# A cross-attention and mixture-of-experts kernel: the order of its first loads, a projection in three passes, and new priorities in its opening list

## Chip, cores and metric

The kernel runs on one core of one Trainium2 chip. The metric is device microseconds for one execution of the whole program. The core has a matrix engine (TensorE, "PE" in the profile; its weight loads are "PEld"), a vector engine (VectorE, "DVE"), a scalar engine (ScalarE, "ACT"), a third elementwise engine (GpSimd, "POOL") and a queue engine (SyncE, "SP") that here only issues DMAs. ACT issues a few DMAs as well.

## What is computed

```python
x = x + xattn(layernorm(x), ctx, Wq, bq, Wk, bk, Wv, bv)
x = x + moe(layernorm(x), w_router, w_gating, w_gate, w_up, w_down)

# xattn: q = n @ Wq + bq; k = ctx @ Wk + bk; v = ctx @ Wv + bv
#        softmax(q k^T / 16) v, for each of the 16 batches
# moe:   combine weights from two softmaxes over 8 experts, then for each expert
#        (silu(n @ w_gate[e]) * (n @ w_up[e])) @ w_down[e], weighted and summed
```

x has 16 batches of 112 rows of 256; ctx has 16 batches of 375 rows of 256; each of the 8 experts has 1024 hidden columns. Everything is float32.

## The kernel before

The program has two parts. The **front** is the attention, the second layernorm, the router and the preparation of the first expert weights; it takes about the first 114 us. The **expert part** follows: 128 steps, each of seven block products (Strassen's scheme) of three matmuls, with the down projections between them.

The expert part does not multiply plain float32. Each operand is split into an upper part, rounded to a reduced format that the code calls fp32r, and a lower part, the rest. A product is three matmuls: upper by upper, upper by lower, lower by upper (`PASSES`; `prod`, L454, and `down_group`, L422). The attention's value projection (L1120) does the same. The other products of the front multiply plain float32, and the profile lists each of these matmuls as two instructions.

In the front, Wq and Wk are never applied to x and ctx one after the other. The kernel forms M = Wq Wk^T / 16 once: both weights are transposed on PE (`turned`, L863, tile `ps_w`), multiplied (`joined`, L877, tile `ps_m`), and scaled out of PSUM by ACT (L885) into `m_sb`. For each of four groups of four batches (g = 0 to 3), ACT and DVE normalize x to `xn`; PE transposes it (`turn`, L1001, tile `ps_xT`); ACT or DVE copies the transpose to `xnT_b` (by the helper at L740 to L742); PE multiplies it by M (`project`, L1014, tile `ps_qk`), in two halves `m` with two float32 matmuls of 448 columns each; ACT adds a bias and writes `qk` (L1023). Each batch b then has its ctx transposed (L1059, `ps_cT`), scores (L1071, `ps_sc`), a softmax on DVE and ACT, the transposed probabilities (L1092, `ps_pp`), their product with ctx (L1105, `ps_aa`), the value projection (L1120, `ps_po`), the residual and the second layernorm (L1127 to L1161), and one more transpose (L1167, `ps_xx`). `route(h)` computes the router's logits for half h of the rows (L1199, `ps_lg`) and what follows on ACT and DVE (L1210 to L1237); `split` forms upper and lower parts of the experts' input blocks (L295 on ACT, L298 on POOL).

The order of all this is not written out by hand. A planner, class `Line`, takes each operation with its engine (or a choice of two, `EITHER`), an estimated cost, a priority `pri`, what it reads and writes, and which ring buffers it needs. A load may be given an estimated landing time, `lands`. `Line.run` repeatedly takes the operation that can start first; among those of one engine that can start by then, the lowest `pri` wins. `LAG` is the estimated delay of a hand-over from another engine. The result is one fixed order per engine, which the hardware runs in order. The eight PSUM banks, and buffers for ctx, `xnT` and others, are such rings.

At the very start PE has nothing to multiply. It runs `WARM` = 7 matmuls on zeros (`idle`, L817), and up to `FILL` = 5 more of them are put where the planner sees a gap after the transposes of Wq. Loads of the start, in order of issue: SP has batches 0 and 1 of x (L799), Wq, Wk (L771), ctx of batches 0 and 1 (L794, L795), group 1 of x (L787), Wv; ACT has bq, bk and bv (L768) and then batches 2 and 3 of x (L799). Rows bq and bv are spread over all partitions by a matmul with ones and an ACT copy (`spread`, L839 and L841).

Of the kernel before, what the change touches and what calls it, by code (L numbers as in the profile page):

```python
# [30 lines left out]
class Line:  # L31


    LAG = {"PE": 0.2, "SP": 0.1}
    SECOND = 0.5

    def __init__(self, rings):
# [106 lines left out]
def kernel(  # L144
# [104 lines left out]
        + [ctx_t[7][:, m * GT : (m + 1) * GT]]  # L249
        for m in range(KC)  # L250
    ]
    xnT_b = [wide[6][:, k * GT : (k + 1) * GT] for k in range(KC)]
    x1_b = [wide[6][:TQ, KC * GT + i * D : KC * GT + (i + 1) * D] for i in range(3)]
    x1T = [wide[i].rearrange("p (k t) -> p k t", k=KC) for i in (2, 7)]
    s_b = [buf("s", [P, N], f"s{i}") for i in range(11)]
# [4 lines left out]
    wT = buf("d", [P, 2, KC, D], "wT")  # L260
    wv_hi, wv_lo = wv_b[:, 0], wv_b[:, 1]
    mix = buf("d", [P, 4, D], "mix")
    m_sb, bv_b, v_b = mix[:, :KC], mix[:, KC], mix[:, KC + 1]
    b_b = buf("rawd", [P, 2, D], "b_b")
    wv = buf("rawd", [P, KC, D], "wv")

# [530 lines left out]
    def load_x0(queue, i):  # L797
        t = own(xg_b, ("xg", 0))[0]
        queue.dma_start(t[:, i : i + 2, :], x[i : i + 2].rearrange("b t d -> t b d"))  # L799

    def x_loaded(g):
        if g:
            op("SP", 0.45 if g < 3 else 0.9, 4 * g - 6, lambda: load_x(g), new=(("xg", ("xg", g)),),
               waits=(("ctx", 5), ("ctx", 6)) if g == 3 else (), kb=448)
            return
        op("SP", 0.45, -22, lambda: load_x0(nc.sync, 0), writes=("x0",), new=(("xg", ("xg", 0)),), kb=224, lands=4.1)
        op("ACT", 0.45, -18, lambda: load_x0(nc.scalar, 2), writes=(("xg", 0),), kb=224, lands=5.5)

    def ctx_loaded(b):
        op("SP", 0.85, b - 3.5, lambda: load_ctx(b), new=(("ctx", ("ctx", b)),), kb=375)  # L810


    WARM, FILL = 7, 5

    def idle(k, n):
        for _ in range(n):
# [1 line left out]

    op("PE", 0.43 * WARM + 1.2, -50, lambda: idle(0, WARM), new=(("bank", ("idle", 0)),), writes=("warm",))
    x_loaded(0)  # L820
    load(-19, 256, lambda: weight(nc.sync, wn[:, 0], Wq), "wn0", lands=4.7)
    load(-18, 256, lambda: weight(nc.sync, wn[:, 1], Wk), "wn1", lands=7.0)
    load(-20, 1, lambda: row(nc.scalar, b_b[:, 0], bq), "bq0", queue="ACT", lands=3.0)
    load(-20, 1, lambda: row(nc.scalar, b_b[:, 1], bk), "bk0", queue="ACT", lands=3.3)
    load(-20, 1, lambda: row(nc.scalar, bv_b, bv), "bv0", queue="ACT", lands=3.6)
    op("ACT", 1.5, -16, lambda: nc.scalar.activation(warm, nhalf, AF.Exp), writes=("exp",))
    ctx_loaded(0)
    ctx_loaded(1)
    load(-1.9, 256, lambda: weight(nc.sync, wv, Wv), "wv")
    load(1.0, 16, load_router, "wr")  # L830
    for b in range(2, B):
# [4 lines left out]
    def spread(name, t, pri):  # L836

        k = ("b", name)
        op("PE", 0.45, pri, lambda: nc.tensor.matmul(bank(k, [P, D]), ones[:1], t[:1], start=True, stop=True),  # L839
           reads=(name + "0",), new=(("bank", k),))  # L840
        op("ACT", 0.38, pri, lambda: nc.scalar.copy(t, bank(k, [P, D])), reads=(k,), writes=(name,))  # L841

    spread("bq", b_b[:, 0], -24)
    spread("bv", bv_b, -23)

    def turn_bias():
        for j in range(KC):
# [24 lines left out]
    def joined(i):  # L872
        k = ("m", i)

        def join():
            for j in range(KC):
                nc.tensor.matmul(  # L877
                    bank(k, [P, D + 1]), wT[:, 0, j, i * P : (i + 1) * P], wk_b[:, j, :],
                    start=(j == 0), stop=(j == KC - 1),
                )  # L880

        op("PE", 0.87, -9, join, reads=["bkc"] + [("wT", s, j) for s in range(2) for j in range(KC)],
           new=(("bank", k),))
        op("ACT", 0.37, -9,
           lambda: nc.scalar.activation(m_sb[:, i, :], bank(k, [P, D + 1])[:, :D], AF.Copy, scale=SCALE),  # L885
           reads=(k,), writes=("m",))
        op("ACT", 0.2, -8,
           lambda: nc.scalar.activation(warm[:, i : i + 1], bank(k, [P, D + 1])[:, D:], AF.Copy, scale=SCALE),
           reads=(k, "exp"), writes=(("v", i),))
        op("DVE", 0.25, -5, lambda: nc.vector.tensor_scalar_mul(v_d[:, i, :], ident, warm[:, i : i + 1]),  # L890
           reads=(("v", i),), writes=(("vd", i),), port=True)
# [64 lines left out]

    def group(g):

        pri = 4 * g - 2.5 if g else -6
        at = slice(g * G, (g + 1) * G)  # L960
        xt = lambda i: x_at(g, i)

# [43 lines left out]
        for k in range(KC):  # L1006
            op("PE", 0.4, pri, lambda k=k: turn(k), reads=(("xn", g, 0), ("xn", g, 1)),
               new=(("bank", ("xT", g, k)),))
            op(EITHER, (0.54, 0.6), pri, lambda e, k=k: copy_on(e, xnT_b[k], bank(("xT", g, k), [P, GT])),
               reads=(("xT", g, k),), new=((f"xnT{k}", ("xnT", g, k)),))  # L1010

        def project(m):
            for k in range(KC):
                nc.tensor.matmul(  # L1014
                    bank(("qk", g, m, 0), [P, GT]), m_sb[:, k, m * P : (m + 1) * P], xnT_b[k],
                    start=(k == 0), stop=(k == KC - 1),
                )

        for m in range(KC):
            op("PE", 1.51, pri, lambda m=m: project(m), reads=("m", ("xnT", g, 0), ("xnT", g, 1)),  # L1020
               new=(("bank", ("qk", g, m, 0)),))
            op("ACT", 0.63, pri,
               lambda m=m: nc.scalar.activation(  # L1023
                   own(qk_b[m], ("qk", g, m)), bank(("qk", g, m, 0), [P, GT]), AF.Identity,
                   bias=r_sb[:, m : m + 1]),
               reads=(("qk", g, m, 0), "r"), new=((f"qk{m}", ("qk", g, m), (0, 1, 0, 2)[g]),),
               waits=(("ctx", 7),) if g == 3 else ())
# [6 lines left out]
            )  # L1034

        for i in range(G):
            op("DVE", 0.52, pri + 0.5, lambda i=i: bias(i), reads=(("xn", g, i // 2), "v"), writes=(("c0", g),),
               port=True)
        op("DVE", 0.22, pri + 0.5,
           lambda: nc.vector.tensor_scalar(cs[:TQ, at], cs[:TQ, at], bqk_b[:TQ], None, op0=ALU.add),  # L1040
# [2 lines left out]
    def batch(b):  # L1043
# [18 lines left out]
                )  # L1062

        for k in range(KC):
            op("PE", 0.33, b + 0.6, lambda k=k: turn(k), reads=(("ctx", b),), new=(("bank", ("cT", b, k)),))
            op(EITHER, (0.45, 0.53), b + 0.6, lambda e, k=k: copy_on(e, ctT(k), bank(("cT", b, k), [P, TK])),
               reads=(("cT", b, k),), new=(("ctT", ("ctT", b, k)),))

        def score():
# [3 lines left out]
                    start=(k == 0), stop=(k == KC - 1),  # L1073
                )

        op("PE", 1.33, b, score, reads=(("ctT", b, 0), ("ctT", b, 1), ("qk", g, 0), ("qk", g, 1)),
           new=(("bank", ("sc", b), *some),))
        op("DVE", 0.57, b,
           lambda: nc.vector.reduce_max(top(), bank(("sc", b), [TQ, TK]), axis=AX.X, negate=True),
# [27 lines left out]
                        start=(c == 0), stop=(c == NK - 1),  # L1107
                    )

        op("PE", 1.35, b, mix_ctx, reads=(("pT", b), ("ctx", b)), new=(("bank", ("aa", b), *some),))  # L1110
        op(EITHER, (0.36, 0.4), b, lambda e: copy_on(e, aT()[:, 0], bank(("aa", b), [P, KC, TQ])),
           reads=(("aa", b),), new=(("aT", ("aT", b)),))
        op("DVE", 0.41, b,
# [3 lines left out]
        def project():  # L1117
# [4 lines left out]
                        start=(k == 0 and s == 0), stop=(k == KC - 1 and s == 2),  # L1122
                    )

        op("PE", 0.75, b, project, reads=(("aT", b), ("aTl", b), "wvb"), new=(("bank", ("po", b), *some),))
        op("DVE", 0.5, b,
           lambda: nc.vector.scalar_tensor_tensor(  # L1127
               x1(), bank(("po", b), [TQ, D]), total[:TQ, col], x_at(g, i),
               op0=ALU.mult, op1=ALU.add),
# [18 lines left out]
        op("DVE", 0.95, b, stats, reads=(("x1", b),), writes=(("va1", b),))  # L1148
# [5 lines left out]
        def norm():  # L1154
# [8 lines left out]
        op("ACT", 0.55, b - 0.5, norm, reads=(("x1", b), ("nm1", b)), new=(("x1n", ("x1n", b)),))  # L1163

        def turn_x1():
            for k in range(KC):
# [4 lines left out]
        op("PE", 0.21, b, turn_x1, reads=(("x1n", b),), new=(("bank", ("xx", b), *some),))  # L1171
# [19 lines left out]
    def route(h):  # L1191

        key = ("lg", h)
        pri = (9.3, 21)[h]
        lg = lgs[h]

        def logits(j):
# [60 lines left out]
    route(0)  # L1258
    for h in range(NH):
        for i in (X_A11, X_A12):  # L1260
            split(h, i, (6.5, 28)[h], *early(h))
# [169 lines left out]
```

## Time and profile before

| | us |
|---|---|
| median of 3 runs | 962.53 (962.35 to 962.54) |
| the profiled execution | 962.02 |
| its span, first to last instruction | 960.24 |
| PE busy in the span | 954.9 |
| DVE, ACT, POOL busy | 646.9, 609.2, 376.5 |

The profiled execution is 0.5 us below the median, and 1.8 us of it lie outside the span. A matmul's end is modelled in this profile, and the durations of neighbouring matmuls overlap: what one of them costs is read from the distance of starts, or from the chain of waits, which puts one after the other. The busy time of the engines in the front, by stretches of it:

```profile
20.00:30.00 10.00, 10.00 (x64) 7.76 (x63) 7.20 (x27) 6.04 (x16) 4.18 (x6) 1.00 1.06 260
30.00:40.00 10.00, 10.00 (x74) 8.47 (x74) 6.68 (x30) 9.02 (x25) 4.69 (x7) 1.00 0.65 186
40.00:50.00 10.00, 10.00 (x62) 7.55 (x61) 8.28 (x31) 7.51 (x20) 4.46 (x6) 1.00 0.43 126
50.00:60.00 10.00, 10.00 (x73) 8.52 (x73) 5.19 (x18) 6.92 (x19) 3.35 (x4) 1.00 0.39 110
60.00:70.00 10.00, 10.00 (x86) 9.49 (x85) 7.83 (x29) 5.94 (x17) 2.11 (x3) 1.00 0.08 24
70.00:80.00 10.00, 10.00 (x59) 7.24 (x58) 8.85 (x27) 8.45 (x22) 7.28 (x9) 1.00 0.05 13
80.00:90.00 10.00, 10.00 (x74) 8.61 (x73) 7.76 (x31) 6.88 (x20) 7.76 (x13) 1.00 0.04 12
90.00:100.00 10.00, 10.00 (x74) 8.68 (x72) 7.65 (x26) 7.93 (x21) 9.84 (x16) 1.00 0.30 89
```

The columns are the stretch, its length, the busy time (and number of instructions) of PE, PEld, DVE, ACT and POOL, the granted PE clock, the share of the 16 DMA engines that was busy, and GB/s.

### The profile page before, as it was taken

Reading aid. Unit: us, or ns where it says so; the run is one execution under the profiler, and the core shown is the slowest. Engines: PE = TensorE matmul, PEld = TensorE weight load, DVE = VectorE, ACT = ScalarE, POOL = GpSimd, SP = SyncE. Lnnn points to the kernel's source line nnn. Section 1 sums busy time; section 2 is a strip of 40 time slices with the busy share of each in tenths; the row PEclk is TensorE's granted clock in tenths of the full one; section 3 lists DMA queues with packets and bytes.
Section 4 is the critical chain, followed back from the end, with each engine's and each line's share of the span. In section 5 each row is a group of like instructions: output and inputs, shape, how many; then the busy total and the mean of one; then the engine's idle time right before and its main releaser. Section 6 shows DMA issues by size and latency. Waiting matters only on the chain.

```text
span 960.2 us, 16096 instructions
## 1 busy us (share of the span) xinstructions
PE 954.9 (99%) x6066; PEld 894.2 (93%) x6066; DVE 646.9 (67%) x1290; ACT 609.2 (63%) x1241; POOL 376.5 (39%) x481
## 2 busy tenths in 40 slices
PE   9999999999999999999999999999999999999998
PEld 5887899999999999999999999999999999999998
DVE  4868686777675666756676757667666767566675
ACT  4867776666666666666556665666566666666553
POOL 3428963444315443344334333543244431544000
PEclk9999999999999999999999999999999999999999
DMA  8621201011101110011100110111001110100001
GB/s 225 183 70 38 64 23 34 23 34 45 34 12 33 33 45 23 12 34 44 34 23 24 36 41 23 34 34 33 23 24 33 44 33 12 33 24 12 19 21 39
DMA packets 36067, 38.65 MB, mean 40 GB/s; under 512 B 3267, under 2 KB 33990, under 8 KB 35990
## 3 DMA queue, kind: packets, MB, share of 16 engines
q1 hardware_dynamic: 35744, 37.40, 13.4%
q8 instruction: 47, 0.77, 0.4%
q14 instruction: 30, 0.25, 0.1%
q10 hardware_dynamic: 246, 0.23, 0.1%
HBM read 33.95 MB, written 1.84 MB: 37 GB/s over the span
## 4 chain that ended last, share of the span: by engine, by line
PE 99%; DVE 0%; issue 0%; ACT 0%
PE pd L422 32%; PE pC L454 16%; PE pE L454 16%; PE pA L454 16%; PE pB L454 8%; PE ps_aa L1105 2%; PE ps_sc L1071 2%; PE ps_qk L1014 1%; PE ps_po L1120 1%; PE ps_cT L1059 1%; PE ps_lg L1199 1%; PE ps_idle L817 1%; PE ps_pp L1092 1%; PE ps_xx L1167 0%; PE ps_xT L1001 0%; PE ps_m L877 0%
## 5 line engine op out<-in xcount | busy, mean ns | idle before, releaser
L422 PE MATMUL pd<-wd,hhi 128*128 128x256 f32 x1792 | 311.2, 277 | 0.0
L422 PEld LDWEIGHTS pd<-wd,hhi 128*128 128x128 f32 x1792 | 275.9, 188 | 1.9
L422 PE MATMUL pd<-wd,hlo 128*128 128x256 f32 x896 | 248.4, 277 | 0.0
L454 PE MATMUL pC<-xs_hi,w 128*128 128x448 f32 x508 | 184.8, 364 | 0.1
L454 PE MATMUL pE<-xs_hi,w 128*128 128x448 f32 x508 | 184.5, 363 | 0.0
L454 PE MATMUL pA<-xs_hi,w 128*128 128x448 f32 x504 | 183.3, 364 | 0.0
L357 POOL TENSOR_TENSOR w<-raw,w 128x384 fp32r<-128x384 f32 x64 | 78.4, 1225 | 265.4 <-ACT w L347 265.4
L422 PEld LDWEIGHTS pd<-wd,hlo 128*128 128x128 f32 x896 | 168.4, 188 | 0.0
L648 ACT COPY pB<-pA 128x448 f32<-128x448 f32 x122 | 63.8, 523 | 104.0 <-PE pA L454 104.0
L366 POOL TENSOR_TENSOR wd<-rawd,wd 128x512 fp32r<-128x512 f32 x32 | 41.5, 1298 | 180.1 <-ACT wd L364 180.1
L454 PEld LDWEIGHTS pC<-xs_hi,w 128*128 128x128 f32 x508 | 95.3, 188 | 10.9 <-DVE s_1c L568 0.5
L454 PEld LDWEIGHTS pE<-xs_hi,w 128*128 128x128 f32 x508 | 95.4, 188 | 6.9 <-ACT pE L585 0.4
L454 PEld LDWEIGHTS pA<-xs_hi,w 128*128 128x128 f32 x504 | 94.6, 188 | 5.6
L658 ACT COPY pE<-pB 128x448 f32<-128x448 f32 x122 | 63.1, 517 | 54.2 <-DVE s_6s L528 0.8
L454 PE MATMUL pC<-xs_lo,w 128*128 128x448 f32 x254 | 91.9, 362 | 0.0
L454 PE MATMUL pE<-xs_lo,w 128*128 128x448 f32 x254 | 91.5, 360 | 0.0
L454 PE MATMUL pB<-xs_hi,w 128*128 128x448 f32 x252 | 91.4, 363 | 0.0
L454 PE MATMUL pA<-xs_lo,w 128*128 128x448 f32 x252 | 90.7, 360 | 0.0
L357 POOL TENSOR_TENSOR w<-tt,w 128x512 fp32r<-128x512 f32 x64 | 88.0, 1375 | 0.1
L454 PEld LDWEIGHTS pE<-xs_lo,w 128*128 128x128 f32 x254 | 47.6, 187 | 3.4
L454 PEld LDWEIGHTS pB<-xs_hi,w 128*128 128x128 f32 x252 | 47.3, 188 | 3.1
L454 PEld LDWEIGHTS pC<-xs_lo,w 128*128 128x128 f32 x254 | 47.6, 187 | 2.5
(1453 smaller groups left out, 1772.0 us busy)
## 6 DMA issues: line engine op xcount, KB each, us to landing
raw<-in_L_ffn_w_gate_dram SPq DMA_DIRECT2D x32, 256.0 KB
raw<-in_L_ffn_w_up_dram SPq DMA_DIRECT2D x32, 256.0 KB
rawd<-in_L_ffn_w_down_dram SPq DMA_DIRECT2D x32, 256.0 KB
ctx<-in_ctx_dram SPq DMA_DIRECT2D x13, 336.0 KB
out_dram<-acc SPq DMA_DIRECT2D x6, 256.0 KB
wide<-in_ctx_dram SPq DMA_DIRECT2D x3, 336.0 KB
wide<-in_x_dram SPq DMA_DIRECT2D x2, 448.0 KB
ctx<-in_ctx_dram SPq DMA_DIRECT2D x13, 39.0 KB
```

What stands on the lines that cost most here:

```text
L357: nc.gpsimd.tensor_sub(wts[k][1][:, d], w, f(wts[k][0][:, d]))
L366: nc.gpsimd.tensor_sub(wds[q][1], rawds[q], f(wds[q][0]))
L422: nc.tensor.matmul(pd, hs[a][:, t * P : (t + 1) * P], wds[q][w][:, fi, :], start=(opening and s == 0), stop=(last and s == 2), skip_group_ ...
L454: nc.tensor.matmul(ps, w_[w][:, wi, :], (xs_hi, xs_lo)[a][h][xi], start=(start and s == 0), stop=(stop and s == 2), skip_group_check=True,)
L648: nc.scalar.copy(pb, pa)
L658: nc.scalar.copy(pe, pb)
L817: nc.tensor.matmul(bank(("idle", k), [P, 512]), zero[:, :P], zero, start=True, stop=True)
L1014: nc.tensor.matmul(bank(("qk", g, m, 0), [P, GT]), m_sb[:, k, m * P : (m + 1) * P], xnT_b[k], start=(k == 0), stop=(k == KC - 1),)
L1059: nc.tensor.transpose(bank(("cT", b, k), [P, TK])[:, c * KT : (c + 1) * KT], ct()[:, c, k * P : (k + 1) * P], ident[:KT, :KT],)
L1071: nc.tensor.matmul(bank(("sc", b), [TQ, TK]), own(qk_b[k], ("qk", g, k))[:, i * TQ : (i + 1) * TQ], ctT(k), start=(k == 0), stop=(k == KC ...
L1092: nc.tensor.transpose(bank(("pp", b), [KT, NK, TQ])[:, c, :], p()[:, c * KT : (c + 1) * KT], ident[:TQ, :TQ])
L1105: nc.tensor.matmul(bank(("aa", b), [P, KC, TQ])[:, k, :], ct()[:, c, k * P : (k + 1) * P], pT()[:, c, :], start=(c == 0), stop=(c == NK - 1),)
```

## The change

**Loads.** Wq moves from SP to ACT, ahead of bq and bk there. Batches 2 and 3 of x move from ACT to SP, ahead of Wk. bv is no longer loaded as a row and spread by PE and ACT; one DMA on SP, after ctx of batch 1, writes it to all 128 partitions. The estimated landing times of bq and bk become later, and the spread of bq gets the priority of the bk step beside it.

**Zero matmuls.** `WARM` goes from 7 to 8, `FILL` from 5 to 6.

**The queries' projection.** M and the transposed `xn` are each held as an upper and a lower part, in tiles that the expert part uses only later. ACT writes M's upper part, DVE its lower part. The copy of the transpose becomes the upper part, and a new DVE operation per transpose writes the lower part. `project` runs six matmuls in place of two float32 ones (which the profile lists as four instructions), for each of two halves in each of four groups.

**The planner's numbers.** The PE hand-over is taken as 0.15 for 0.2, and a number of priorities change; the later ones among them are the turns of ctx, the scores and the first router step, the earlier ones most of what ends a batch.

```diff
-    LAG = {"PE": 0.2, "SP": 0.1}
+    LAG = {"PE": 0.15, "SP": 0.1}
...
-    xnT_b = [wide[6][:, k * GT : (k + 1) * GT] for k in range(KC)]
+    xnT_b = [[t[1][5 + k][:, :GT] for t in (xs_hi, xs_lo)] for k in range(KC)]
+    m_b = [[t[1][3 + k][:, :D] for t in (xs_hi, xs_lo)] for k in range(KC)]
...
-        op("ACT", 0.45, -18, lambda: load_x0(nc.scalar, 2), writes=(("xg", 0),), kb=224, lands=5.5)
+        op("SP", 0.45, -22, lambda: load_x0(nc.sync, 2), writes=(("xg", 0),), kb=224, lands=5.5)
...
-    WARM, FILL = 7, 5
+    WARM, FILL = 8, 6
...
-    load(-19, 256, lambda: weight(nc.sync, wn[:, 0], Wq), "wn0", lands=4.7)
+    load(-21, 256, lambda: weight(nc.scalar, wn[:, 0], Wq), "wn0", queue="ACT", lands=4.7)
     load(-18, 256, lambda: weight(nc.sync, wn[:, 1], Wk), "wn1", lands=7.0)
-    load(-20, 1, lambda: row(nc.scalar, b_b[:, 0], bq), "bq0", queue="ACT", lands=3.0)
-    load(-20, 1, lambda: row(nc.scalar, b_b[:, 1], bk), "bk0", queue="ACT", lands=3.3)
-    load(-20, 1, lambda: row(nc.scalar, bv_b, bv), "bv0", queue="ACT", lands=3.6)
+    load(-20, 1, lambda: row(nc.scalar, b_b[:, 0], bq), "bq0", queue="ACT", lands=4.4)
+    load(-20, 1, lambda: row(nc.scalar, b_b[:, 1], bk), "bk0", queue="ACT", lands=5.2)
...
+    load(-2.2, 128, lambda: nc.sync.dma_start(bv_b, bv.rearrange("(o d) -> o d", o=1).to_broadcast([P, D])), "bv")
...
-    spread("bq", b_b[:, 0], -24)
-    spread("bv", bv_b, -23)
+    spread("bq", b_b[:, 0], -9.7)
...
-           lambda: nc.scalar.activation(m_sb[:, i, :], bank(k, [P, D + 1])[:, :D], AF.Copy, scale=SCALE),
-           reads=(k,), writes=("m",))
+           lambda: nc.scalar.activation(m_b[i][0], bank(k, [P, D + 1])[:, :D], AF.Copy, scale=SCALE),
+           reads=(k,), writes=(("mh", i),))
+        op("DVE", 0.42, -9,
+           lambda: nc.vector.scalar_tensor_tensor(
+               m_b[i][1], bank(k, [P, D + 1])[:, :D], SCALE, f(m_b[i][0]), op0=ALU.mult, op1=ALU.subtract),
+           reads=(k, ("mh", i)), writes=("m",))
...
+            op("DVE", 0.54, pri,
+               lambda k=k: nc.vector.tensor_sub(xnT_b[k][1], bank(("xT", g, k), [P, GT]), f(xnT_b[k][0])),
+               reads=(("xT", g, k), ("xnT", g, k)), writes=(("xnl", g, k),))
 
         def project(m):
             for k in range(KC):
-                nc.tensor.matmul(
-                    bank(("qk", g, m, 0), [P, GT]), m_sb[:, k, m * P : (m + 1) * P], xnT_b[k],
-                    start=(k == 0), stop=(k == KC - 1),
-                )
+                for s, (a, w) in enumerate(PASSES):
+                    nc.tensor.matmul(
+                        bank(("qk", g, m, 0), [P, GT]), m_b[k][a][:, m * P : (m + 1) * P], xnT_b[k][w],
+                        start=(k == 0 and s == 0), stop=(k == KC - 1 and s == 2),
+                    )
 
         for m in range(KC):
-            op("PE", 1.51, pri, lambda m=m: project(m), reads=("m", ("xnT", g, 0), ("xnT", g, 1)),
+            op("PE", 1.21, pri, lambda m=m: project(m),
+               reads=("m", *(("xnT", g, k) for k in range(KC)), *(("xnl", g, k) for k in range(KC))),
...
```

The priorities, `pri` before and after (b is the batch, g the group):

| operation | before | after |
|---|---|---|
| normalization, transposes, projection of group g > 0 | 4g - 2.5 | 4g - 3.0 |
| key-bias sums of a group (DVE) | pri + 0.5 | pri + 1.0 |
| turn of ctx, on PE | b + 0.6 | b + 1.3 |
| scores, on PE | b | b + 0.6 |
| probabilities by ctx (L1105) | b | b - 0.4 |
| residual, its statistics (DVE) | b | b - 0.3 |
| second layernorm (ACT) | b - 0.5 | b - 1.0 |
| transpose of its result (L1167) | b | b - 0.5 |
| router of the first half | 9.3 | 13.5 |
| first two splits of the first half | 6.5 | 8 |

More of the change, by code (lines that the diff above doesn't have):

```diff
@@ L262 @@
     mix = buf("d", [P, 4, D], "mix")
-    m_sb, bv_b, v_b = mix[:, :KC], mix[:, KC], mix[:, KC + 1]
+    bv_b, v_b = mix[:, KC], mix[:, KC + 1]
     b_b = buf("rawd", [P, 2, D], "b_b")
@@ L957, in group @@
     def group(g):
-        pri = 4 * g - 2.5 if g else -6
+        pri = 4 * g - 3.0 if g else -6
         at = slice(g * G, (g + 1) * G)
@@ L1008, in group @@
                new=(("bank", ("xT", g, k)),))
-            op(EITHER, (0.54, 0.6), pri, lambda e, k=k: copy_on(e, xnT_b[k], bank(("xT", g, k), [P, GT])),
+            op(EITHER, (0.54, 0.6), pri, lambda e, k=k: copy_on(e, xnT_b[k][0], bank(("xT", g, k), [P, GT])),
                reads=(("xT", g, k),), new=((f"xnT{k}", ("xnT", g, k)),))
+            op("DVE", 0.54, pri,
+               lambda k=k: nc.vector.tensor_sub(xnT_b[k][1], bank(("xT", g, k), [P, GT]), f(xnT_b[k][0])),
+               reads=(("xT", g, k), ("xnT", g, k)), writes=(("xnl", g, k),))
         def project(m):
             for k in range(KC):
-                nc.tensor.matmul(
-                    bank(("qk", g, m, 0), [P, GT]), m_sb[:, k, m * P : (m + 1) * P], xnT_b[k],
-                    start=(k == 0), stop=(k == KC - 1),
-                )
+                for s, (a, w) in enumerate(PASSES):
[3 more added lines that the diff above has]
+                    )
         for m in range(KC):
-            op("PE", 1.51, pri, lambda m=m: project(m), reads=("m", ("xnT", g, 0), ("xnT", g, 1)),
+            op("PE", 1.21, pri, lambda m=m: project(m),
+               reads=("m", *(("xnT", g, k) for k in range(KC)), *(("xnl", g, k) for k in range(KC))),
                new=(("bank", ("qk", g, m, 0)),))
@@ L1036, in group @@
         for i in range(G):
-            op("DVE", 0.52, pri + 0.5, lambda i=i: bias(i), reads=(("xn", g, i // 2), "v"), writes=(("c0", g),),
+            op("DVE", 0.52, pri + 1.0, lambda i=i: bias(i), reads=(("xn", g, i // 2), "v"), writes=(("c0", g),),
                port=True)
@@ L1064, in batch @@
         for k in range(KC):
-            op("PE", 0.33, b + 0.6, lambda k=k: turn(k), reads=(("ctx", b),), new=(("bank", ("cT", b, k)),))
+            op("PE", 0.33, b + 1.3, lambda k=k: turn(k), reads=(("ctx", b),), new=(("bank", ("cT", b, k)),))
             op(EITHER, (0.45, 0.53), b + 0.6, lambda e, k=k: copy_on(e, ctT(k), bank(("cT", b, k), [P, TK])),
@@ L1074, in score @@
                 )
-        op("PE", 1.33, b, score, reads=(("ctT", b, 0), ("ctT", b, 1), ("qk", g, 0), ("qk", g, 1)),
+        op("PE", 1.33, b + 0.6, score, reads=(("ctT", b, 0), ("ctT", b, 1), ("qk", g, 0), ("qk", g, 1)),
            new=(("bank", ("sc", b), *some),))
@@ L1108, in mix_ctx @@
                     )
-        op("PE", 1.35, b, mix_ctx, reads=(("pT", b), ("ctx", b)), new=(("bank", ("aa", b), *some),))
+        op("PE", 1.35, b - 0.4, mix_ctx, reads=(("pT", b), ("ctx", b)), new=(("bank", ("aa", b), *some),))
         op(EITHER, (0.36, 0.4), b, lambda e: copy_on(e, aT()[:, 0], bank(("aa", b), [P, KC, TQ])),
@@ L1123, in project @@
                     )
-        op("PE", 0.75, b, project, reads=(("aT", b), ("aTl", b), "wvb"), new=(("bank", ("po", b), *some),))
-        op("DVE", 0.5, b,
+        op("PE", 0.75, b + 0, project, reads=(("aT", b), ("aTl", b), "wvb"), new=(("bank", ("po", b), *some),))
+        op("DVE", 0.5, b - 0.3,
            lambda: nc.vector.scalar_tensor_tensor(
@@ L1146, in stats @@
             nc.vector.tensor_scalar_mul(nm1[:TQ, col], mv1[:TQ, b, 0:1], -1.0)
-        op("DVE", 0.95, b, stats, reads=(("x1", b),), writes=(("va1", b),))
+        op("DVE", 0.95, b - 0.3, stats, reads=(("x1", b),), writes=(("va1", b),))
         op("POOL", 0.56, b - 4,
@@ L1162, in batch @@
            reads=(("rs1", b),), writes=(("nm1", b),))
-        op("ACT", 0.55, b - 0.5, norm, reads=(("x1", b), ("nm1", b)), new=(("x1n", ("x1n", b)),))
+        op("ACT", 0.55, b - 1.0, norm, reads=(("x1", b), ("nm1", b)), new=(("x1n", ("x1n", b)),))
         def turn_x1():
@@ L1169, in turn_x1 @@
                 )
-        op("PE", 0.21, b, turn_x1, reads=(("x1n", b),), new=(("bank", ("xx", b), *some),))
+        op("PE", 0.21, b - 0.5, turn_x1, reads=(("x1n", b),), new=(("bank", ("xx", b), *some),))
         h, at = divmod(b, HB)
@@ L1193, in route @@
         key = ("lg", h)
-        pri = (9.3, 21)[h]
+        pri = (13.5, 21)[h]
         lg = lgs[h]
@@ L1260 @@
         for i in (X_A11, X_A12):
-            split(h, i, (6.5, 28)[h], *early(h))
+            split(h, i, (8, 28)[h], *early(h))
     for n, i in enumerate((X_S1, X_S2, X_S3, X_S4)):
```

## Prediction

> **What bounds the kernel now.** I read the page first: who is busy, and what ended last.
>
> ```profile
> PE 954.9 (99%) x6066; PEld 894.2 (93%) x6066; DVE 646.9 (67%) x1290; ACT 609.2 (63%) x1241; POOL 376.5 (39%) x481
> ...
> PE 99%; DVE 0%; issue 0%; ACT 0%
> ```
>
> PE is on the chain for 99% of the span. The waits listed for PE agree: apart from 1.2 us at the start they name two, of 0.4 and 0.2 us. So time comes from PE's work, from PE's start, and from the few breaks in its chain. The change touches only the front, so next I read the chain of waits in order of time from 0 to 119 us. Columns: start, us, what.
>
> ```profile
> 1.19 3.17 PE ps_idle L817 x7
> 4.36 1.15 PE ps_b_bq L839 x2
> 5.50 0.85 PE ps_b_bv L839 x2
> 6.36 1.05 PE ps_w L863 x4
> 7.40 0.94 PE ps_bk L848 x4
> 8.34 2.26 PE ps_idle L817 x5
> 10.61 0.04 issue
> 10.65 1.11 PE ps_w L863 x4
> ...
> 16.63 3.01 PE ps_qk L1014 x8
> ...
> 34.71 1.51 PE ps_qk L1014 x4
> ...
> 110.10 0.63 DVE s_0u L1320
> 110.73 0.02 issue
> 110.76 0.63 DVE s_0c L1320
> 111.39 0.04 issue
> 111.43 0.88 PE ps_first_C L454 x3
> ```
>
> From 10.65, where Wk's transposes begin, the chain is PE alone up to 110.08. Behind that lie breaks of 2.2 us: three DVE additions of 0.63 and an ACT copy of 0.35 (112.63). A matmul saved between 10.65 and 110 is therefore saved in the end, as long as PE stays fed.
>
> **The projection on PE.** On the chain the four groups' `ps_qk` cost 3.01, 1.51 + 1.52, 1.52 + 1.52 and 3.01: 12.09 us for 32 instructions, 0.377 each. The new form, fp32r of 128x448, stands in the trace: the chain has "PE pA L454 x3" at 0.60 throughout the first expert steps, 0.20 each. Four groups by two halves by six are 48, or 9.6 us. Entering such a block from float32 costs something: on the chain the first blocks between float32 work took 0.62, 0.70, 0.62 and 0.72, on average 0.06 to 0.07 over 0.60. For eight blocks that is 0.5 us, for four (halves back to back) 0.25. Saving: 12.09 - 9.6 = 2.5 at best, 2.0 at worst; I take **2.1**.
>
> [...] The rows say 2.5: an fp32r matmul of 448 columns costs 0.20, not half of 0.377. [...]
>
> **What the projection adds elsewhere.** DVE gets eight subtractions of 128x448, PSUM less SBUF. The nearest row is L1320, an addition with one operand in PSUM in the same shape, 614 to 622 ns: 5.0 us. Two lower parts of M, 128x256, are like L1127 (112x256, 0.48): 1.0. Together 6.0 us on DVE, of which the table above shows 44.0 us busy between 20 and 80, so 16 idle. This hides as a sum, but not everywhere: in 70 to 80, where group 3 is projected, DVE has 8.85 and ACT 8.45, and 1.2 more makes ten of ten. Against that the router of the first half leaves this stretch (L1214 to L1237, nine DVE operations of 0.17 to 0.34, about 2.2 us), as its priority becomes 13.5. I cost DVE's load at nothing.
>
> As a delay, each group's projection starts a subtraction (0.62) and a hand-over later. What covers it is PE work that needs neither: turns of ctx (0.32 each), `ps_pp` (0.32), `ps_aa` (1.33). In group 1 the last copy of the transpose ended at 34.30 and the matmuls began at 34.55, so the delay would show there if nothing else were ready; in group 3 the copies ended at 72.88, the matmuls began at 73.68. Cost with cover: nothing. Without it: 4 x 0.65 = 2.6 us.
>
> **The start.** WARM + 1 adds 0.43: the loads of L817's weights stand 0.43 apart (1.59, 2.02, 2.44, 2.87). bv's spread goes: -0.85. FILL + 1 adds 0.43 again. Wq's transposes and bk keep their price. Sum: 0.43 - 0.85 + 0.43 = 0.0, and Wk's transposes begin at 10.65 once more, if Wk is there and all six zero matmuls are placed ahead of it. Was it Wk or the fill that PE waited for?
>
> ```profile
> PEld ps_w L863 <- PE ps_idle L817: 1.0, 1, 1.0
> ```
>
> In the list of waits of the first 20 us the name is that of the zero matmuls, not of a DMA. So Wk landed no later than that, and the fill is what sets 10.65.
>
> *DMA.* Ahead of Wk the same 960 KB must pass (x in two parts of 224, Wq, Wk of 256 each), in another order: SP issues x's second part at 1.20 in Wq's place, Wk at 1.67 as before, Wq goes out on ACT at 0.73 and is needed after bq's spread, near 5.9. Worst case: x's second part, so far shared between two queues (it landed at 8.7, where DVE's L909 starts), goes wholly ahead of Wk, 224 KB at the 250 GB/s of this stretch, 0.9 us. Best case: none, even a gain if not all fills are placed: down to -0.9. I take 0, by the wait row. x's second part lands earlier, which lets DVE's statistics start earlier, but PE is not waiting for them.
>
> *bq and bk* now stand behind Wq in ACT's queue. PE reads bq at 4.8, and the order puts bk behind Wq's transposes. Should bq be late, PE waits in order, and the six fills behind it move along: at most 0.5.
>
> *bv's DMA* is 128 KB: 0.5 us of DMA time, on a stretch where the DMA share is about 1.0. Behind it on SP stand group 1's x, Wv and the later ctx. SP also waits for landings (3.2 us before 8.71, for x), so Wv and x may issue some us later than 4.6 and 5.0. Who waits: group 1's statistics (14.7, wanted for a projection at 34), Wv's cast (17.0, wanted at 31), ctx of batch 2 (turned after 19.6). Nobody soon: nothing. Uncovered: 0.5. POOL reads bv first at 18.96.
>
> *The clock.* [...]
>
> ```profile
> L877 PE MATMUL ps_m<-wide,wT x8: 378/380/670, 11.8 to 13.6; 128*128 128x257 f32 x8
> ```
>
> One of eight took 670 ns, the other seven 380. With the same pattern ending at the same 10.65 I expect the same moment, near 12.3. [...]
>
> **Priorities.** They add no work. With PE gapless from 10.65 to 110 they can only make gaps or move those behind 110. Later turns and scores and earlier ends of batches shorten the way to the last batch, and the router's 28 logits of the first half (2.8 us on PE between 61 and 71) become work that can fill a gap later. On the other side fewer turned ctx lie ready when PE wants one. The 2.2 us of breaks behind 110 come from the expert part's first additions, which stay. Bounds: -1.5 to +1.5; value: 0.
>
> **Sum.** 960.2 - 2.1 = 958.1 for the span; 1.8 outside makes 959.9 against the profiled execution's 962.0. The median lies 0.5 above that: **960.4**. Its own range is 958.9 to 961.9. What can be told from no change here is 0.2%, 1.9 us, so the border to faster is at 960.6, and this forecast lies close by it.
>
> **Rivals.**
> *Breaks go as well (958.2).* The priorities remove half or all of the 2.2 us behind 110. For it: PE would have logits left over. Against it: those additions wait for products in a fixed sequence.
> *Given back (962.6).* PE saves 2.1 but waits for the lower parts, 2.6 uncovered at worst less some cover, or the start slips by 0.9 and the breaks grow. For it: group 1's 0.25 us between copy and matmul. Against it: five cT turns followed in a row at 24.4, so PE has spare work as a rule.
> *DVE becomes the bound (966.4), slower.* In the front all softmax, residual and statistics work goes through DVE in one fixed order; 6.0 us added to it and shown in full give 960.4 + 6.0. It decides from the point where 4.1 of the 6.0 are exposed. For it: 70 to 80 is full, and POOL reaches 9.84 of 10 behind it. Against: 16 us idle between 20 and 80, and `EITHER` copies can go to ACT.
>
> **Numbers.** Forecast 0.50 (0.34 of it below 960.6, 0.16 within 0.2%); breaks gone too 0.16 (all faster); given back 0.16 (0.04 faster, 0.09 same, 0.03 slower); DVE 0.18 (all slower). Faster 0.54, same 0.25, slower 0.21. The range reaches down to 957.4 (breaks gone, and 0.8 of the start's possible gain) and up to 965.0, where 4.6 of DVE's 6.0 us are exposed; some 0.15 to 0.2 lies outside, most of it DVE's case in full.
>
> **What would show it.** Right: `ps_qk` on the chain near 2.4 us a group; Wk's transposes near 10.65; PE with no new waits up to 108; the last `ps_first` blocks some 2 us earlier. Wrong: PE waiting for DVE ahead of L1014 or in batches; a later 10.65; M's product at half rate; or longer breaks at 108 to 116.

## The result and the profile after

The changed kernel is slower. Its median is 965.52 us (22 runs, 962.40 to 969.97); the kernel before, run beside it on the same chip, has 962.47 (22 runs, 959.56 to 962.90). The ratio is 1.004, with a 95% interval of 1.0029 to 1.0051.

The times of the changed kernel fall into two groups with nothing between 964.3 and 966.7: 11 runs from 962.4 to 964.3, and 11 from 966.8 to 970.0. So the median is no run's time; it lies halfway across the gap, and one run more in either group would move it by more than 1 us. The kernel before has two groups as well, closer together (5 runs from 959.6 to 960.7, 17 from 962.0 to 962.9), and its profile is of the upper one. The profiled execution of the changed kernel, 963.12 with a span of 961.1, is from its lower group, so its profile can show only part of the loss. The upper group needed a profile of its own (below).

First the page of the changed kernel: busy time of the engines, and the chain's shares.

```profile
PE 952.0 (99%) x6082; PEld 896.9 (93%) x6082; DVE 658.5 (69%) x1298; ACT 609.4 (63%) x1242; POOL 377.5 (39%) x481
...
PE 98%; DVE 2%; issue 0%; ACT 0%; DVEq 0%; ACTq 0%
```

PE is busy 2.9 us less (954.9 before), and the span is 0.9 us longer: PE now waits somewhere. DVE's share of the chain went from nothing to 2%, and DVE is busy 11.6 us longer, where the prediction's sum was 6.0. The list of PE's waits gives the place (columns: who waited for whom; us in total, times, longest):

```profile
PE ps_xx L1177 <- DVE total L1109: 3.4, 1, 3.4
```

There was no such wait before. The timeline there (start, us, engine, line, operation, tile written and read, shape):

```profile
85.17 0.55 POOL L1160 TENSOR_TENSOR rs<-rs,nhalf 112x1 f32<-112x1 f32 x1
...
85.47 4.75 DVE L1225 TENSOR_TENSOR lg<-lg,lmx 128x112 f32<-128x112 f32 x1
85.69 1.00 POOL L359 TENSOR_TENSOR w<-raw,w 128x384 fp32r<-128x384 f32 x1
...
88.82 1.26 POOL L359 TENSOR_TENSOR w<-tt,w 128x512 fp32r<-128x512 f32 x1
90.04 0.49 POOL L334 TENSOR_TENSOR tt<-raw 128x128 f32<-128x128 f32 x1
...
90.14 0.53 DVE L744 COPY s<-ps_cT 128x375 f32<-128x375 f32 x1
...
90.82 0.61 PE L1177 MATMUL ps_xx<-ident,x1n 112*128 112x112 f32 x2 [3.36 <-DVE total L1109]
```

One DVE instruction takes 4.75 us. It is the router's subtraction for the first half, over 112 columns; its twin in the kernel before (L1215) took 0.28 at 71.2. Both instructions of that line, and POOL beside the first, in the kernel before:

```profile
70.48 0.92 POOL L1150 TENSOR_TENSOR rs<-rs,nhalf 112x1 f32<-112x1 f32 x1 [2.67 <-DVE nm L1146]
...
71.24 0.28 DVE L1215 TENSOR_TENSOR lg<-lg,lmx 128x112 f32<-128x112 f32 x1
71.37 0.73 POOL L996 TENSOR_TENSOR ctx<-ctx,mix 112x256 f32<-112x256 f32 x1
...
114.27 1.44 DVE L1215 TENSOR_TENSOR lg<-lg,lmx 128x112 f32<-128x112 f32 x1
114.29 1.29 POOL L357 TENSOR_TENSOR w<-tt,w 128x512 fp32r<-128x512 f32 x1
```

After the change it began while a short POOL instruction was running, and ended when the four L359 instructions behind that on POOL, 85.69 to 90.1, were done. (L359 is L357 of the kernel before.) POOL itself went on without a gap, with L334 at 90.04. And in the kernel before POOL was not idle at 71.24 either, yet the subtraction was not held there; beside L357 at 114.27 it was. So it matters what POOL runs, not only that it is busy: 0.28 us beside L1150 and L996, 1.44 beside L357. Behind the held subtraction, in DVE's fixed order, stand a reciprocal (`total`, L1109) and copies that PE wants, and so PE is idle for 3.4 us.

What follows the idle time costs more. Busy time by stretch (columns as in the table of stretches before: PE, PEld, DVE, ACT, POOL, then the granted PE clock):

```profile
84.00:88.00 4.00, 3.46 (x25) 2.74 (x24) 3.86 (x8) 3.63 (x10) 3.92 (x7) 1.00 0.14 37
88.00:92.00 4.00, 1.18 (x6) 1.04 (x7) 3.96 (x7) 0.40 (x2) 3.92 (x7) 0.83 0.38 123
92.00:96.00 4.00, 4.00 (x22) 3.59 (x22) 3.30 (x13) 2.73 (x9) 1.59 (x4) 0.74 0.01 4
```

The granted clock falls to 0.83 and then to 0.74. In stretches of 1 us it is 0.84 from 90 to 91, 0.50 from 91 to 94 and 0.96 from 94 to 95: PE ran at half rate for 3.4 us. It was busy from 90.82 on, so this takes about 0.5 x (94.1 - 90.8) = 1.6 us. With the 3.4 of idling it makes 5.0.

Against this loss stand a gain at the start and the projection's. The start in the chain of the profiled execution:

```profile
1.19 3.59 PE ps_idle L819 x8
...
6.82 1.40 PE ps_idle L819 x6
8.22 0.29 PE ps_w L864 x2
...
9.24 2.00 PE ps_m L878 x8
...
14.05 2.66 PE ps_qk L1023 x12
```

Six zero matmuls take 1.40 us here, 0.23 each, where five took 2.26 before, their weight loads 0.43 apart (8.27, 8.68, 9.11, 9.53): PE came to full rate near 5.3, not near 12.2. (These times are those at which the clock record in each trace begins, 5.34 and 12.21. Ahead of it the trace has no record, and the clock column reads 1.00. The pace agrees: M's eight matmuls take 2.00 us here, 380 ns each, and before one of them, at 11.8, took 670.) `ps_qk` now begins at 14.05 instead of 16.63. Over the four groups it takes 10.11 us on the chain instead of 12.09.

### The profile page after: what moved, and what is told of

It is laid out like the page before. It is cut to its first block, busy times and chain, and to the rows that moved or that the text cites. A ratio compares the mean times of both kernels' runs of the same rounds, so it can differ in the third digit from the quotient of the medians.

```text
span 961.1 us, 16135 instructions
## 1 busy us (share of the span) xinstructions
PE 952.0 (99%) x6082; PEld 896.9 (93%) x6082; DVE 658.5 (69%) x1298; ACT 609.4 (63%) x1242; POOL 377.5 (39%) x481
## 4 chain that ended last, share of the span: by engine, by line
PE 98%; DVE 2%; issue 0%; ACT 0%; DVEq 0%; ACTq 0%
PE pd L424 32%; PE pC L456 16%; PE pE L456 16%; PE pA L456 16%; PE pB L456 8%; PE ps_aa L1115 2%; PE ps_sc L1081 2%; PE ps_po L1130 1%; PE ps_qk L1023 1%; PE ps_cT L1069 1%; PE ps_lg L1209 1%; PE ps_idle L819 1%; DVE lg L1225 0%; PE ps_pp L1102 0%; DVE wide L289 0%; PE ps_xx L1177 0%
## 5 line engine op out<-in xcount | busy, mean ns | idle before, releaser
L359 POOL TENSOR_TENSOR w<-raw,w 128x384 fp32r<-128x384 f32 x64 | 78.3, 1224 | 268.5 <-ACT w L349 268.5
L456 PEld LDWEIGHTS pC<-xs_hi,w 128*128 128x128 f32 x508 | 95.3, 188 | 11.6 <-DVE s_1c L570 0.8
L359 POOL TENSOR_TENSOR w<-tt,w 128x512 fp32r<-128x512 f32 x64 | 87.9, 1374 | 0.1
```

Source lines behind the costliest of these rows:

```text
L359: nc.gpsimd.tensor_sub(wts[k][1][:, d], w, f(wts[k][0][:, d]))
L456: nc.tensor.matmul(ps, w_[w][:, wi, :], (xs_hi, xs_lo)[a][h][xi], start=(start and s == 0), stop=(stop and s == 2), skip_group_check=True,)
```

## The experiments

I took as landmark the first matmul of `pC` behind the wait for `s_1c`, where the expert part starts in earnest (117.76 before, 118.21 after). Behind it the program has the same work in every kernel; to the last instruction it took 840.6 to 842.9 us, and one and the same kernel had both: the changed kernel 842.9 and 840.6 in two profiles that agree to 0.14 us at the landmark. What makes this spread of 2 us is open; it is as large as the distance of the two groups of the kernel before. Differences of two profiles are therefore read at the landmark, and times from many runs.

**The changed kernel again,** to meet the upper group in a profile.

> The changed kernel once more, for a second profile, since its 22 times fall in two groups, 962.4 to 964.3 and 966.8 to 970.0, and the first profile is of the lower one. Lock theory (the router's subtraction on DVE, 4.75 us for 0.28, waits while POOL works, and PE loses 3.4 us behind it): an execution of the upper group shows the same or another DVE instruction held for some 6 us more, and PE idle behind it. Clock theory: it shows PE at half rate for some us longer at the start, and the front shifted as a whole. Load theory (the 6 us of new DVE work): no single long instruction, but many short waits of PE for DVE.

Measured: median 963.96 (22 runs, 961.03 to 969.02), ratio 1.0028 (1.0018 to 1.0039). Again two groups, now 17 to 5, but the profiled execution fell in the lower one; it has the same subtraction of 4.75 us and the same gap of 3.4 us. How far the median is from that of before depends on how many runs fall in the upper group; slower it is in both sessions.

**The router's place.** First the changed kernel with the router's old priority, then the old kernel with the new one.

```diff
-        pri = (13.5, 21)[h]
+        pri = (9.3, 21)[h]
```

> The changed kernel with the first router step's priority back at 9.3. Lock theory: the subtraction is placed where POOL is less busy, takes about 0.3 us, PE's gap near 87 us goes; median 959 to 961, and the times near 969 go too. Load theory: DVE's added work is still there, the median stays at 964 to 966. Clock theory: still two groups 6 us apart.

> The kernel before with that priority alone moved to 13.5. Lock theory: the subtraction meets POOL's chain of weight operations, is held for some us, and the kernel gets 2 to 6 us slower (964 to 968). Load theory and clock theory: no change beyond 1 us from the kernel before (961.5 to 963.5).

Measured for the router put back: 961.78 (14 runs), ratio 1.0012 (0.9994 to 1.003), a little above the 959 to 961 expected. The subtraction is at 66.3 and takes 276 ns, PE's gap of 3.4 us is gone, and the landmark comes at 116.11, 2.1 earlier than after. Two groups remain (seven runs from 958.5 to 960.6, six from 965.3 to 965.6, and one at 962.94), so the times near 965 have another cause. DVE still has all six microseconds of new work, so that work as such doesn't cause the gap. PE has other waits in place of it (0.5 for `ps_aa`, 0.5 for `ps_xx`, 0.4 for `ps_lg`, 0.2 for `ps_first_C`), and the granted clock is 0.80 and 0.77 in 108 to 112 and 112 to 116 (a block of three expert matmuls takes 1.12 us at 111.66, 0.60 at 116.99): the router at its old place isn't free in the new order.

Measured for the late router alone: 964.38 (10 runs), ratio 1.0024 (1.0015 to 1.0034). The old kernel has now got a held subtraction. From its timeline:

```profile
90.54 2.55 DVE L1215 TENSOR_TENSOR lg<-lg,lmx 128x112 f32<-128x112 f32 x1
90.74 1.00 POOL L357 TENSOR_TENSOR w<-raw,w 128x384 fp32r<-128x384 f32 x1
91.70 1.27 POOL L357 TENSOR_TENSOR w<-tt,w 128x512 fp32r<-128x512 f32 x1
...
93.61 0.57 PE L1071 MATMUL ps_sc<-s,ctx 128*112 128x375 f32 x1 [1.72 <-DVE s L742]
```

This POOL chain has two long instructions, the other had four, and the subtraction is held until the end of each. (POOL had run the short L1150 from 90.23.) One number in the list of priorities is enough to slow the old kernel.

**Same place, another operand.** This kernel leaves the changed kernel's priorities as they are. In the first half the maximum and the subtraction read the logits in PSUM, not ACT's copy in SBUF; what is computed is the same. If the late place as such were the cause, nothing should change. If it is two SBUF operands beside a busy POOL, the hold should go.

```diff
-            nc.vector.reduce_max(lmx, lg, axis=AX.X)
-            nc.vector.tensor_sub(lg, lg, lmx.unsqueeze(3).to_broadcast([P, NTT, 2, E]))
+            src = lg if h else bank(key, [P, NTT, 2 * E]).rearrange("p j (s e) -> p j s e", s=2)
+            nc.vector.reduce_max(lmx, src, axis=AX.X)
+            nc.vector.tensor_sub(lg, src, lmx.unsqueeze(3).to_broadcast([P, NTT, 2, E]))
```

> The changed kernel, whose first subtraction of the router reads its logits from PSUM and no longer from the copy in SBUF; PE's order is nearly the same. Lock theory, in the form that the wait is for a read path shared with POOL: with one operand in PSUM the instruction takes about 0.3 us although POOL is as busy, PE's gap goes, median 959 to 961. If DVE is held by POOL for another reason (the write, or POOL's load as such), it stays at several us and the time at 963 to 969. Load theory: no change from the changed kernel.

Measured: 960.30 (22 runs), ratio 0.9987 (0.9975 to 0.9999), against 1.0028 for the changed kernel in the same session. The subtraction by its line (instruction count; ns minimum, median, maximum; start), and the same three stretches:

```profile
L1226 DVE TENSOR_TENSOR lg<-ps_lg,lmx x1: 276/276/276, 85.5 to 85.5; 128x112 f32<-128x112 f32 x1
```

```profile
84.00:88.00 4.00, 4.00 (x31) 3.45 (x31) 3.36 (x14) 3.83 (x11) 3.92 (x7) 1.00 0.14 37
88.00:92.00 4.00, 4.00 (x27) 3.19 (x27) 3.79 (x15) 3.10 (x11) 3.92 (x7) 1.00 0.40 127
92.00:96.00 4.00, 4.00 (x31) 3.45 (x30) 3.22 (x12) 2.43 (x7) 3.92 (x7) 1.00 0.04 8
```

Same instruction, same moment (85.5), POOL as busy as after (3.92 of 4.00 in the first two stretches), and 276 ns in place of 4,754. PE is busy throughout and its clock stays at 1.00. The landmark comes at 113.22, 5.0 us earlier than after; the 3.4 of idle PE and 1.6 of half rate are gone. This settles the first cause: not the load of DVE, not the place by itself, but where the second operand lies while POOL runs these instructions.

So the runs have both sides: 4.75 us with two operands in SBUF, 0.28 with one. That DVE and POOL share a read path, as the expectation has it, was the author's guess; the runs show the times only. Four L359 went first here, and two L357 in the old kernel with the late router (2.55 us). Why the subtraction is let in ahead of L334 but not between two L359, which follow each other as closely, no run here shows; nor why the old kernel's ran unheld, in 0.28, beside L1150 and L996.

Even so two groups remain, 957.3 to 958.5 (10 runs) and 962.3 to 963.2 (10), with two runs at 960.2 and 960.4. They are another matter.

**The start alone.** The old kernel with the new loads, the DMA of bv and 8 + 6 zero matmuls.

> The kernel before with the new loads, bv's DMA and the zero matmuls (8 and 6) alone. [...] If the recorded sum holds (start worth 0.0): the same two groups as the kernel before, near 959.6 and 962.2, in the same shares.

Measured: 962.11 (22 runs), ratio 1.0016 (1.0006 to 1.0026): ten runs at 959.4 to 959.9, eleven at 962.9 to 964.1, one at 961.29. The kernel before, in the same session, has 5 of 32 runs at 957.9 to 958.6 and the rest at 959.9 to 961.3. So this part of the change alone drives the groups apart, from some 2.3 to some 4 us, and puts nearly half of the runs in the lower one; but neither group is faster than its like. `ps_qk` began at 12.96 in the profiled execution, 3.7 earlier than before, yet the landmark is at 117.18, only 0.6 earlier. Waits of 0.9 and 1.6 us at 109.4 and 115.0 (for `s_0c` from DVE, and for `pE` from ACT), which the shifted order brought, took most of it.

**The projection alone.** The old kernel with the upper and lower parts and the six matmuls.

> The kernel before with the three-pass projection alone. The recorded sum: 2.1 us less in each group, 957.5 and 960.1. Load theory: DVE's 6 us are exposed at least in part, and it is no faster than the kernel before or up to 4 us slower. In the trace, a projection of a group should take 2.45 us on the chain in place of 3.03.

Measured: 962.29 (7 runs), ratio 1.0025 (1.001 to 1.0041). PE's matmuls became cheaper, and the end of the front gave more than that back. Two stretches:

```profile
110.00:114.00 4.00, 2.27 (x13) 1.29 (x11) 1.77 (x3) 1.71 (x5) 3.92 (x7) 1.00 0.24 78
114.00:118.00 4.00, 4.00 (x15) 3.52 (x15) 1.17 (x3) 2.79 (x8) 3.70 (x6) 0.61 0.18 62
```

PE had spent its spare matmuls by 110 and then waited for the last batch: residual on DVE at 108.03, statistics, a power on POOL, normalization on ACT at 112.0, transpose at 112.65. PE's pauses there are 0.2, 1.1 and 0.4 us, none of them long, and yet the clock behind them was 0.61: each block of three expert matmuls took 1.12 instead of 0.60. The landmark is at 119.52, 1.8 later than before. The idling alone doesn't foretell this: in two kernels above, a wait of 1.7 us (late router) left the clock at 1.00 from 92 to 100, and behind one of 1.6 (start alone) the blocks took 0.60 to 0.61. So the projection with the old priorities gains nothing; in the changed kernel PE's chain goes on from 103.92 to 116.56 without a wait. That the new priorities keep PE fed there is likely but not shown: no run changes them alone.

**What makes the second group: the zero matmuls.** If PE's full rate comes early or late by when the zero matmuls fall, other numbers of them should move it. All of these are the kernel with the PSUM operand, with only this line changed:

```diff
-    WARM, FILL = 8, 6
+    WARM, FILL = 16, 0    # then 8, 0; 4, 6; 12, 0
```

> The changed kernel with the PSUM form of the subtraction, 16 zero matmuls at the start and none of the later ones. [...]

> The same kernel with 8 zero matmuls at the start and none of the later six. Fill theory (Wk has landed near 5.2 us, and PE's next work is held by the six zero matmuls alone): Wk's transposes start near 6.7 for 8.06 where the full rate comes early (lower group 956.4 for 957.8) and near 7.9 for 10.4 where it comes late. Against it: without the six, PE is less busy, the full rate comes later, and the share of the upper group grows or its time is no better than 962.7.

Then one more profile each of the changed kernel and of its PSUM form, to meet the upper groups, and two more numbers.

> A third profile of the changed kernel, to meet an execution of its upper group (966.7 to 970). Clock theory: PE's full rate comes near 12 us in place of 5, Wk's transposes start near 10.4 in place of 8.1, and all stages up to the held subtraction lie some 4.5 to 5 us later; the subtraction is held in the same way. If it is another hold: the start is as in the first profile and the extra 5 us lie further on.

> A second profile of the changed kernel with the PSUM form of the subtraction, to meet its upper group (962.3 to 963.2). Clock theory: full rate near 12 us, the front up to 20 us shifted by 4.5 to 5 us against the lower group, no long DVE instruction anywhere.

> The changed kernel with the PSUM form of the subtraction, with 4 zero matmuls at the start in place of 8. [...]

> As with 16 zero matmuls and none later, but 12. [...] 955.5 to 957.5, one group or two less than 3 us apart. It would beat both kernels.

The further profile of the changed kernel is of a run of 967.18 us, an upper one (in that session the kernel before ran some 2 us faster). Its start, from the chain:

```profile
7.92 2.67 PE ps_idle L819 x6
...
11.96 3.79 PE ps_m L878 x8
...
18.72 2.66 PE ps_qk L1023 x12
```

The same six zero matmuls take 2.67 us, and M's product 3.79 where it took 2.00 (a median of 635 ns a matmul for 380): PE stayed at half rate until 16.0. `ps_qk` begins at 18.72, 4.7 later than in the lower group and 2.1 later than before. The subtraction is held here as well (4.746 us). The profile of the kernel with the PSUM operand, 961.19, shows the same start (2.67 and 3.79, full rate near 16.9, `ps_qk` at 19.19) and no held instruction. So the upper group is the late full rate, and each of the two causes occurs without the other. They do add to each other: in the upper run the half rate behind the held subtraction lasted 6.8 us (94.5 to 101.3; twelve matmuls of `ps_aa` took 2.53 us in it, 1.33 after it) in place of 3.4, which costs 1.2 us more. The 4.7 at the start and this 1.2 are the 5.9 us between the two landmarks of the changed kernel (124.09 and 118.21).

| zero matmuls, first and fill | median (runs) | range | ratio (95%) | full rate in the profiles, us |
|---|---|---|---|---|
| 8, 6 | 960.30 (22) | 957.28 to 963.19 | 0.9987 (0.9975 to 0.9999) | 4.7; 16.9 |
| 16, 0 | 956.78 (5) | 956.27 to 958.20 | 0.9965 (0.9952 to 0.9978) | 5.6 |
| 8, 0 | 957.70 (10) | 955.57 to 958.51 | 0.9972 (0.9963 to 0.9981) | 5.1 |
| 4, 6 | 958.24 (22) | 957.85 to 959.31 | 0.9983 (0.9976 to 0.9989) | 10.5 |
| 12, 0 | 956.03 (6) | 955.35 to 956.71 | 0.996 (0.9945 to 0.9975) | 6.3 |

Medians of different sessions don't compare (the kernel before had 962.06, 960.34 and 960.23 in the three); the ratios do. If fewer zero matmuls meant more late starts, 8 with no fill and 4 with 6 would have more of them than 8 with 6. With 8 and no fill all ten runs are in one group; with 4 and 6 all 22 lie within 1.5 us, and the one profile has the full rate at 10.5, between early and late. So fewer zero matmuls do not simply mean more late starts. None of the 21 runs without later zero matmuls lies in an upper group; for each row alone that is weaker, since the changed kernel once had only 5 of 22 runs in its upper group. (Wk, which the expectation for 8 and 0 has at 5.2, landed near 6.0 there.)

What decides between early and late with 8 and 6 isn't shown; the clock records give the moments. In the changed kernel's, the first full rate lasted 85.33 us, the half rate 3.41 and the next full rate 866.99: 25, one and 254 steps of 3.41 us. In its upper run the first full rate lasted 23 such steps (16.0 to 94.5) and the half rate two. In the five profiled executions with 8 and 6 that were early, full rate came between 3.95 and 5.52 us; in the two late ones it came at 15.95 and 16.91, three such steps behind 5.71 and 6.67. With 12 zero matmuls it came at 6.3, and that was early. Seven executions are few, no run sets the moment, and why a late start comes some 10 us behind an early one is open.

The last row, 12 and no fill with the PSUM operand, beats both kernels by its ratio: 0.4% faster than before (0.25 to 0.55), with six runs. Its landmark is at 113.20, that of the lower group above (113.22). It is that group without the late runs.

## Why the prediction was wrong

The forecast was 960.4 in a range of 957.4 to 965.0; the median of 965.52 lies outside, on the other side of the kernel before. By how much is in part luck: the median stood in the gap between two groups of equal size, and in the second session, with other shares, it was 963.96, inside the range. That the change slows the kernel, where a gain was forecast, holds in both. Where the time went, at the landmark, with the start read at the first matmul of `ps_qk`:

| us | start | `ps_qk` | held subtraction | sum | landmark measured |
|---|---|---|---|---|---|
| lower group | 14.05 - 16.63 = -2.58 | -1.98 | 118.21 - 113.22 = +4.99 | +0.43 | +0.45 |
| upper group | 18.72 - 16.63 = +2.09 | -1.98 | 124.09 - 118.30 + 0.40 = +6.19 | +6.30 | +6.33 |

The third column is the changed kernel less the one with the PSUM operand, each in the same group; in the upper one the latter was 0.40 behind when its fourth projection began (80.28 against 79.88), and that is taken off. These differ a little in their order too, so it is not the held instruction to the last tenth. The kernel with the PSUM operand reached the landmark at 113.22, where the start and the projection alone give 117.76 - 2.58 - 1.98 = 113.20. So all other priorities together are worth about nothing. In the lower group 0.45 at the landmark became 1.10 in the time (963.12 less 962.02); the other 0.65 lies behind it, within the 2.2 us of spread there.

**Priorities: this step failed.** "They add no work ... Bounds: -1.5 to +1.5; value: 0." With the router at 13.5 the held instruction costs 5.0 us at the landmark, 3.4 of idle PE and 1.6 of half rate, and 6.2 in the upper group; putting the router back gains 2.1 of them, the PSUM operand all. In the old kernel the move alone costs 2.3 (0.0024 x 962.06). No work was added: an instruction was moved beside another engine's work, and there it took seventeen times as long. The view that could have warned was there: the same line in the second half of the kernel before took 1.44 us instead of 0.28, and POOL was busy 9.84 of 10 in 90 to 100. I read that row as room, not as a neighbour. I even booked the move as relief for DVE in 70 to 80. Without this step the sum would have come out right in sign: with the PSUM operand and all other priorities as they are, the ratio is 0.9987 (0.9975 to 0.9999).

**The start: right sum of parts, wrong assumption under it.** +0.43 - 0.85 + 0.43 = 0.0 holds only at half rate, and for the moment of full rate I took "the same moment, near 12.3". It came near 5.3 or near 16.0, so the start was -2.6 or +2.1, and one kernel does both. The row of a single execution, one matmul of M at 670 ns and seven at 380, was a guide to neither.

**DMA order: worth 0, as reasoned.** The wait row had named the zero matmuls, and Wk's transposes did come behind the last fill, at 8.22 and 10.59. The DMAs went better than the zero I took: Wk landed near 7.1 instead of 8.5 (SP waited 0.6 us for it ahead of the load of 7.12), and x's statistics on DVE began at 5.16 instead of 8.72. PE used this only where the fill was absent (8 and no fill: transposes at 6.60, behind the bk step).

**The projection: right in size.** 2.1 was forecast for the chain, 1.98 measured. 10.11 is the 9.6 plus 0.5 that the row of the expert blocks gave. The eight subtractions took 601 to 627 ns (0.62 was taken), M's two lower parts 0.43 (0.48): 5.8 us together. The held one adds 4.5. The rest of DVE's 11.6 us is a balance: copies went to ACT, but the sixteen key-bias sums (L1041, L1031 before), which read two SBUF operands, took 11.1 us in place of 7.6, single ones up to 1.82 (at 75.79, beside POOL's L300 of 128x448 from 75.06 to 77.33; 0.93 at most before). So DVE was slower beside POOL in other places too; no wait of PE in the list comes from them.

**DVE's load costed at nothing: right, but its rival had the right engine.** The case in which DVE becomes the bound said 966.4 and came nearest in time, by luck. Its mechanism, 6.0 us of work exposed, isn't what happened: with all that work, and the router's operand in PSUM, PE has no gap at 84 to 96. It was one waiting instruction. The delay of hand-overs ahead of the projection didn't show as a wait of PE either. That the breaks behind 110 stay was right in size only: some 1.95 us against 2.2 before (115.66 to 118.21 is 2.55 us, 0.60 of it a block of matmuls). The waits for the first additions (L1320) that were to stay are gone from the chain; PE waits for the next pair (L579 and L570) instead.

## What to carry to other kernels

In a list scheduler's fixed order a priority is not free: before an elementwise operation is moved, look at what the other engine (here POOL beside DVE) does at the new place, and count the operation's SBUF operands (here 4.75 us with two, 0.28 with one). A short operation with an unexplained slow twin elsewhere in the trace (here 1.44 us for 0.28) is the warning. And where PE's rate at the start decides microseconds, judge by the groups of many runs, not by one profile.

## What the runs showed of the hardware

- A DVE subtraction of 128x112 with two SBUF operands, 0.28 us when not held, took 4.75 us beside four POOL instructions L359 of 128x384 and 128x512 and 2.55 beside two (L357 of the old kernel). It wasn't let in between them, where they follow each other without a gap, but was done 0.1 us after the last one, though POOL went on at once with another instruction. Beside POOL's L1150 (112x1) and L996 it took 0.28. With one operand in PSUM it took 0.276 beside the same four.
- PE at half rate: after 3.4 us of idling the granted clock was 0.50 for 3.4 us in one execution and for 6.8 in another. Three pauses of 0.2, 1.1 and 0.4 us within 4 us were followed by 0.61 over the next 4; behind a single one of 1.7 us the clock stayed at 1.00, and behind one of 1.6 a block of three expert matmuls kept its 0.60 us.
- From a start of zero matmuls at 1.19 us, full rate came at 4.0 to 6.3, at 10.5, at 12.2 to 13.7 or at 16.0 to 16.9, by kernel and execution. The clock column reads 1.00 all this while, as the record begins only there; the distances of starts show it (0.43 or 0.23 for a zero matmul). Later changes of the clock stood 85.33 and 3.41 us apart in the changed kernel, 25 steps of 3.41 and one, and 78.5 and 6.8 in its upper run, 23 and two.
